# Four states of 32 channels on the partitions in a selective scan, with dense weights streamed

## The chip, the cores and the metric

The kernel runs on one core of one Trainium2 chip. The core has five engines, each with its own in-order queue: TensorE (PE), VectorE (DVE), ScalarE (ACT), GpSimd (POOL) and SyncE (SP), which here issues every DMA. A wait at the head of a queue holds everything behind it. The metric is device time in microseconds (us) of one execution. All data are float32.

## The reference

Eight images of 256 channels and 32x32 pixels (N = 1024 positions) go through four residual layers, each behind a group norm `_gn` (32 groups). Layer 0 is attention with 8 heads of 64; layers 1 and 2 are 3x3 convolutions 256 to 256; layer 3 is the long one. Cut to what matters:

```python
x = x + _L0_conv_ref(_gn(x), w_qkv, w_out, b_out)   # attention, q and k of unit length
x = x + _L1_conv_ref(_gn(x), scale, sign_w, bias)   # 3x3 conv
x = x + _L2_conv_ref(_gn(x), kernel, bias)          # 3x3 conv
x = x + _L3_conv_ref(_gn(x), ...)
# inside layer 3, xs = _gn(x) as positions x channels
xn = layernorm(xs)                  # over the 256 channels of a position
xc = four branches of 64 channels of xn
def mamba(xs):                      # one branch: 64 in, 128 inner channels, 16 states
    u, z = split(xs @ inw.T)
    u = silu(causal_conv4(u))
    xdbc = u @ xpw.T                # 4 columns for dt, 16 for B, 16 for C
    dt = softplus(xdbc[..., :4] @ dtw.T + dtb)
    # for every inner channel d and state s, along the 1024 positions:
    #   h[d,s] = exp(dt[d] * A[d,s]) * h[d,s] + dt[d] * u[d] * B[s]
    #   y[d]   = sum over s of h[d,s] * C[s]
    y = selective_scan(u, dt, B, C, -exp(alog), D)   # y + u * D
    return (y * silu(z)) @ outw.T
xm = mamba(xc) + skip * xc
# gate from two small convs and a sigmoid; depthwise and pointwise convs (r, then x2);
# attention with 8 heads of 32 over x2; a 512-to-256 projection, layernorm, gelu;
# normalisation, depthwise 3x3, layernorm, projection
```

The scan is the part that the change rewrites: 4 branches x 128 channels x 16 states, each a recurrence over 1024 positions, for 8 images.

## The kernel before

**Tiling.** Channels lie on the 128 partitions, positions along the free dimension. All weights are loaded once and stay in SBUF (`weight`, L72). Work tiles of 128x1156 come from one pool of 20 buffers (`work`, L46). In PSUM [...] two `big` tiles and one `acc` tile take two banks each, two `mm` tiles one bank each. The framework places semaphores itself; an instruction waits for the data it reads, and for the readers of the buffer that it takes over.

**Order.** A Python loop over the images (L938) emits `layer0` to `layer3` for one after another, with the next image's `x` loaded early (L942). Dense products go by halves of 512 positions: `project` (L248) and `conv3x3` (L523 on) fill one `mm` tile per half and output block, and evacuate it. `layer_norm` (L177) takes the mean with a matmul by a constant matrix, subtracts, squares on ACT, sums the squares over channels with 16 matmuls whose stationary operand has 8 columns (L196), then Sqrt on ACT and reciprocal on DVE, a matmul that broadcasts the result (L211), and two multiplications per half.

**The scan** is `mamba` (L562 on), once per branch. Its front: in-projection, causal conv on DVE (L588, L597), silu, projection to B, C and dt (L606), softplus (L622 to L629), du = dt*u (L631). B is stored to DRAM (L611). Then for each of the 16 states, with all 128 inner channels on the partitions and all 1024 positions in one tile:

1. `hs` is loaded with one row of B, broadcast to 128 partitions (L638, SP);
2. ACT computes `da` = exp(dt*A) (L641);
3. TensorE broadcasts the state's row of C into a `big` tile, by a matmul with one column of the weights repeated 128 times (L646);
4. GpSimd multiplies `hs` by du (L653);
5. DVE runs the recurrence in `hs` (L662) and multiplies it by C from PSUM (L663);
6. TensorE adds the result into `acc` by a matmul with the identity (L665).

`spread(s + 1)`, steps 1 to 4 of the next state, is emitted ahead of the scan of state s. At the end come y + u*D (L672), the gate (L676, L677), the output matmul (L680) and the skip (L683). A branch's front isn't emitted before the branch ahead of it has ended.

Of the kernel before, what the change touches and what calls it, by code (L numbers as in the profile page):

```python
# [26 lines left out]

@with_exitstack
def preact_stack(ctx: ExitStack, tc: tile.TileContext, I, out, cols):

# [5 lines left out]
    wp = ctx.enter_context(tc.tile_pool(name="wp", bufs=1))  # L36
    xp = ctx.enter_context(tc.tile_pool(name="xp", bufs=2))
    vp = ctx.enter_context(tc.tile_pool(name="vp", bufs=1))
    tp = ctx.enter_context(tc.tile_pool(name="tp", bufs=20))
    sp = ctx.enter_context(tc.tile_pool(name="sp", bufs=2))  # L40
    ps_big = ctx.enter_context(tc.tile_pool(name="ps_big", bufs=2, space=PSUM))
    ps_acc = ctx.enter_context(tc.tile_pool(name="ps_acc", bufs=1, space=PSUM))
    ps_mm = ctx.enter_context(tc.tile_pool(name="ps_mm", bufs=2, space=PSUM))
    dp = ctx.enter_context(tc.tile_pool(name="dp", bufs=2, space=DRAM))

    def work(name):  # L46
        return tp.tile([P, TW], F32, tag="t", name=name)

    def mm_tile():
        return ps_mm.tile([P, HALF], F32, tag="mm", name="mm")  # L50
# [4 lines left out]
    def acc_tile():  # L55
        return ps_acc.tile([P, N], F32, tag="acc", name="acc")

    def load_x(b):
        xt = xp.tile([P, 2, N], F32, tag="x", name="xt")
        nc.sync.dma_start(out=xt, in_=x_in[b].rearrange("(t p) n -> p t n", p=P))  # L60
        return xt


    x_next = load_x(0)
# [7 lines left out]
    def weight(name, parts=P):  # L72
        src = I[name]
        k = src.shape[0] // parts
        t = wp.tile([parts, k] + list(src.shape[1:]), F32, name="w_" + name)
        for i in range(k):
            nc.sync.dma_start(out=t[:, i], in_=src[i * parts : (i + 1) * parts])
        return t

    wqkv = weight("wqkv")  # L80
    wout = weight("wout")
    wc1 = weight("wc1")
    wc2 = weight("wc2")
    minw = weight("minw")
    mxpw = weight("mxpw")
    moutw = weight("moutw")
    mdtw = wp.tile([36, NB, P], F32, name="mdtw")
    nc.sync.dma_start(out=mdtw[32:36], in_=I["mdtw"])
    rpw = weight("rpw")
    fpw = weight("fpw")  # L90
    ainw = weight("ainw")
    aout = weight("aout")
    fcw = weight("fcw")
    projw = weight("projw")
# [6 lines left out]
    make_identity(nc, ident)  # L101

# [16 lines left out]
    var_w = wp.tile([P, NKT, NKT], F32, name="var_w")  # L119
    nc.gpsimd.memset(var_w, 0.0)  # L120
    for i in range(NKT):
        nc.gpsimd.memset(var_w[:, i, i : i + 1], 1.0 / C)
# [8 lines left out]
    a_neg = wp.tile([P, NB * DS], F32, name="a_neg")  # L131
    nc.scalar.activation(a_neg, vec[:, cols["alog"] : cols["alog"] + NB * DS], AF.Exp)
    nc.vector.tensor_scalar_mul(a_neg, a_neg, -1.0)

    def rsqrt_of(t, eps):

        nc.vector.tensor_scalar_add(t, t, eps)
        nc.scalar.activation(t, t, AF.Sqrt)
        nc.vector.reciprocal(t, t)
# [11 lines left out]
    def group_norm(xt, dsts, view=lambda a: a):  # L151
        mv = channel_stats([xt[:, t] for t in range(2)])
        pg = mm_tile()
# [3 lines left out]
        g = sp.tile([P, 2, 2], F32, tag="g", name="g")  # L157
# [4 lines left out]
        pd = mm_tile()  # L162
        nc.tensor.matmul(pd[:, 0:2], gmat, d, start=True, stop=True)
        rs = sp.tile([P, 2], F32, tag="rs", name="rs")
        nc.vector.tensor_add(rs, g[:, :, 1], pd[:, 0:2])
        rsqrt_of(rs, 1e-5)
# [10 lines left out]
    def layer_norm(srcs, dsts, finish):  # L177

        sq = []
        for t in range(2):  # L180
            sq.append(work("ln_sq"))
        for h in range(2):
            pm = mm_tile()
            for t in range(2):
                nc.tensor.matmul(
                    pm, mean_w, srcs[t][:, HALVES[h]], start=t == 0, stop=t == 1
                )
            for t in range(2):
                nc.vector.tensor_sub(dsts[t][:, HALVES[h]], srcs[t][:, HALVES[h]], pm)
                nc.scalar.activation(  # L190
                    sq[t][:, HALVES[h]], dsts[t][:, HALVES[h]], AF.Square
                )
        pv = mm_tile()
        for i in range(NKT):
            for t in range(2):
                nc.tensor.matmul(  # L196
                    pv[0:NKT, 0:P],
                    var_w[:, i],
                    sq[t][:, i * P : (i + 1) * P],
                    start=i == 0 and t == 0,  # L200
                    stop=i == NKT - 1 and t == 1,
                )
        rs = sp.tile([NKT, P], F32, tag="ln_rs", name="ln_rs")
        nc.vector.tensor_scalar_add(rs, pv[0:NKT, 0:P], 1e-5)
        nc.scalar.activation(rs, rs, AF.Sqrt)
        nc.vector.reciprocal(rs, rs)
        for h in range(2):
            pr = mm_tile()
            for i in range(4):
                blk = h * 4 + i  # L210
                nc.tensor.matmul(  # L211
                    pr[:, i * P : (i + 1) * P],
                    ident[0:NKT, blk : blk + 1].to_broadcast([NKT, P]),
                    rs,
                    start=True,
                    stop=True,
                )
            for t in range(2):
                part = dsts[t][:, HALVES[h]]
                nc.vector.tensor_mul(part, part, pr)  # L220
                finish(t, part)

# [25 lines left out]
    def project(w, srcs, evac):  # L248

        last = len(srcs) - 1  # L250
        for m in range(2):
            for h in range(2):
                ps = mm_tile()
                for k, src in enumerate(srcs):
                    nc.tensor.matmul(  # L255
                        ps,
                        w[:, k, m * P : (m + 1) * P],
                        src[:, HALVES[h]],
                        start=k == 0,
                        stop=k == last,  # L260
                    )
                evac(m, HALVES[h], ps)

    def attention_exact(heads):
# [25 lines left out]
        def transposes(u):  # L290
            ps = acc_tile()
# [8 lines left out]
        def values(u):  # L300
            head, qt = u["head"], u["qt"]
            if qt % 4 == 0:
                head["acc"] = mm_tile()
# [23 lines left out]
    def note(sums):  # L327
# [3 lines left out]
        nc.vector.tensor_reduce(chk[:, 0, at : at + 1], sums, axis=AX.X, op=ALU.min)  # L331
        nc.vector.tensor_reduce(chk[:, 1, at : at + 1], sums, axis=AX.X, op=ALU.max)

    def attention(pairs, add_up):
# [4 lines left out]

        def scores(u):  # L340
            pair, h, kt, n = u["pair"], u["h"], u["kt"], u["n"]
            s = acc_tile() if n % 3 == 2 else big_tile()
# [12 lines left out]
        def values(u):  # L355
            pair, h, kt = u["pair"], u["h"], u["kt"]
            if kt == 0:
                pair["acc"] = mm_tile()
# [20 lines left out]
            {"pair": pair, "h": h, "kt": kt} for pair in pairs for h in range(2) for kt in range(NKT)  # L379
        ]  # L380
        for n, u in enumerate(units):
            u["n"] = n
        for n in range(len(units) + 2):
            for stage, at in ((scores, n), (values, n - 2)):
                if 0 <= at < len(units):
                    stage(units[at])


    def layer0(xt, exact=False):
        xn = [work("xn0"), work("xn1")]  # L390
        group_norm(xt, [t[:, 0:N] for t in xn])

        v = vp.tile([P, NKT, 512], F32, tag="v", name="v")

        def values(kt):
            ps = mm_tile()
            for c in range(2):
                nc.tensor.matmul(
                    ps,
                    xn[c][:, kt * P : (kt + 1) * P],  # L400
                    wqkv[:, c, 1024:1536],
                    start=c == 0,
                    stop=c == 1,
                )
            nc.vector.tensor_copy(v[:, kt], ps)

        def rows_of(first, name):

            a = work(name)
            ss = sp.tile([P, 2], F32, tag="ss", name="ss", bufs=4)  # L410
            for h in range(2):
                ps = mm_tile()
                for c in range(2):
                    nc.tensor.matmul(  # L414
                        ps,
                        wqkv[:, c, first : first + P],
# [4 lines left out]
                nc.vector.tensor_copy(a[:, HALVES[h]], ps)  # L421
            sq = work("sq")
            nc.scalar.activation(
                sq[:, 0:N], a[:, 0:N], AF.Square, accum_out=ss[:, 0:1]
            )
            nc.scalar.activation(ss[:, 1:2], ss[:, 0:1], AF.Sqrt)
            nc.vector.tensor_scalar_max(ss[:, 1:2], ss[:, 1:2], 1e-12)
            nc.vector.reciprocal(ss[:, 1:2], ss[:, 1:2])
            return a[:, 0:N], ss[:, 1:2]

        qs, ks = [], []
        for t in range(4):
            q, rq = rows_of(t * P, "q")
            k, rk = rows_of(512 + t * P, "k")
            nc.vector.tensor_scalar(q, q, rq, 10.0, ALU.mult, ALU.mult)
            nc.vector.tensor_scalar_mul(k, k, rk)
            qs.append(q)
            ks.append(k)
            for kt in (2 * t, 2 * t + 1):
                values(kt)  # L440
# [3 lines left out]
        def heads():  # L444
            for t in range(4):
                o.append(work("o"))
                for e in range(2):
                    yield head(t, e)

        def head(t, e):  # L450
# [3 lines left out]
            def take(half, acc):  # L454
# [3 lines left out]
                "q": qs[t][rows],  # L458
# [606 lines left out]
```

## Time and profile before

| | us |
|---|---|
| median of 2 runs | 9570.62 (9567.94 to 9573.3) |
| profiled execution, its own time | 9565.23 |
| its span, first to last instruction | 9563.5 |
| one image to the next | 1195 |
| of that: layer 0, from its first statistics to the first conv | 211 |
| layers 1 and 2 (two convs) | 140 |
| norm and layer norm at the head of layer 3 | 16 |
| four branches of the scan | 531 |
| the rest of layer 3 | 299 |

The stages are those of image 1, cut at the first instruction of each, with some us of overlap at the seams; their sum is 1197. The largest groups outside the lines shown with the prediction:

| line, engine | what | instructions | busy us | mean ns |
|---|---|---|---|---|
| L665 PE | y += hs by the identity | 2048 records | 1211.6 | 726 |
| L360 PE | attention, values | 4096 records | 1098.0 | 617 |
| L646 PE | C broadcast | 2048 records | 1076.3 | 655 |
| L533 PE | 3x3 convs | 2304 records | 1033.5 | 612 |
| L641 ACT | exp(dt*A) | 512 | 563.7 | 1142 |
| L374 DVE | attention, sum of the exponentials | 384 | 470.5 | 1225 |

A float32 matmul leaves two records[...]. Busy time of PE overlaps with its weight loads (PEld), so the two aren't added. In a line of the profile, `hs<-a,hs 128x1024` names output and inputs and the shape in partitions x elements; "idle before" is the time that the engine stood still just before it, with what ended it.

### The profile page before, as it was taken

The numbers are of one execution on the slowest core, as the hardware profiler recorded it, in microseconds if no ns is written. First come the engines' busy times: TensorE is split into PE (matmuls) and PEld (weight loads), VectorE is DVE, ScalarE is ACT, GpSimd is POOL, SyncE is SP. The second block draws the span as 40 slices with busy tenths as digits, with TensorE's granted clock in tenths as the row PEclk, the third lists the DMA queues.
The fourth block names the chain that finished last, engine by engine and source line by source line (L and its number), as shares of the span: only waits on it lengthen the run. The fifth ranks groups of instructions, "written<-read, shape, count | busy, mean of one in ns | idle before, by whom it ended". The sixth has DMA issues, their size and how long they took to land.

```text
span 9563.5 us, 51820 instructions
## 1 busy us (share of the span) xinstructions
PE 7354.8 (77%) x19650; PEld 2690.0 (28%) x19650; DVE 5074.7 (53%) x4146; ACT 2543.9 (27%) x2835; POOL 2190.2 (23%) x1021
## 2 busy tenths in 40 slices
PE   9767897678975789757897578976789757897577
PEld 2322233222332223322233222332223322233222
DVE  6466364663646636466364663646536465364653
ACT  3121331213312133121331213312133121331213
POOL 0253002530025300253002530025300252002520
PEclk9878998788987889878898788987889878898788
DMA  1111001110012100121001210012100121001210
GB/s 51 36 64 42 0 9 36 69 38 2 8 36 69 38 0 9 36 69 38 3 7 36 69 38 5 5 36 71 36 9 0 36 71 36 5 1 36 71 36 5
DMA packets 86139, 300.76 MB, mean 31 GB/s; under 512 B 9844, under 2 KB 12532, under 8 KB 85368
## 3 DMA queue, kind: packets, MB, share of 16 engines
q1 hardware_dynamic: 85880, 297.36, 9.1%
q8 instruction: 156, 2.56, 0.1%
q14 instruction: 103, 0.84, 0.0%
HBM read 286.83 MB, written 10.49 MB: 31 GB/s over the span
## 4 chain that ended last, share of the span: by engine, by line
PE 59%; DVE 23%; issue 9%; POOL 4%; ACT 4%; DMA 0%; DVEq 0%; POOLq 0%; ACTq 0%
PE mm L533 11%; PE mm L360 10%; DVE hs L662 10%; PE big L344 7%; PE acc L665 5%; PE mm L255 4%; PE big L646 4%; PE acc L344 4%; PE mm L414 3%; DVE hs L663 2%; POOL hs L653 2%; DVE u L597 1%; DVE dw L920 1%; PE mm L606 1%; PE mm L716 1%
## 5 line engine op out<-in xcount | busy, mean ns | idle before, releaser
L665 PE MATMUL acc<-hs,ident 128*128 128x512 f32 x2048 | 1211.6, 726 | 1257.2 <-DVE hs L663 1256.9
L653 POOL TENSOR_TENSOR hs<-a,hs 128x1024 f32<-128x1024 f32 x512 | 1887.5, 3715 | 250.5 <-DMA hs<-b_rows 230.2
L662 DVE TENSOR_TENSOR_SCAN hs<-da,hs 128x1024 f32<-128x1024 f32 x512 | 1826.0, 3598 | 219.6 <-POOL hs L653 204.4
L360 PE MATMUL mm<-p,v 128*64 128x512 f32 x4096 | 1098.0, 617 | 0.0
L646 PE MATMUL big<-u,w_mxpw 128*128 128x512 f32 x2048 | 1076.3, 655 | 0.0
L533 PE MATMUL mm<-im,w_wc 128*128 128x512 f32 x2304 | 1033.5, 612 | 29.2 <-DVE im L168 25.6
L641 ACT ACTIVATE da<-dt,a_neg 128x1024 f32<-128x1024 f32 x512 | 563.7, 1142 | 1648.0 <-DVE hs L662 1460.9
L352 ACT ACTIVATE p<-big 128x1024 f32<-128x1024 f32 x688 | 702.4, 1023 | 1014.4 <-PE big L344 1013.4
L665 PEld LDWEIGHTS acc<-hs,ident 128*128 128x128 f32 x2048 | 437.2, 224 | 1894.3 <-DVE hs L663 1447.0
L663 DVE TENSOR_TENSOR hs<-hs,big 128x1024 f32<-128x1024 f32 x512 | 616.8, 1207 | 422.6 <-PE big L646 415.5
L344 PE MATMUL big<-q,k 32*128 32x512 f32 (+1 forms) x2752 | 772.1, 639 | 0.0
L646 PEld LDWEIGHTS big<-u,w_mxpw 128*128 128x128 f32 x2048 | 455.3, 224 | 650.8 <-issue 650.8
L533 PEld LDWEIGHTS mm<-im,w_wc 128*128 128x128 f32 x2304 | 450.4, 196 | 600.4 <-issue 600.4
L762 DVE COPY o<-mm 32x512 f32<-32x512 f32 x128 | 87.6, 684 | 879.6 <-PE mm L360 838.1
L696 POOL MEMSET v<- 128x2048 f32 x8 | 14.4, 1804 | 2195.1 <-PE mm L360 2195.1
L374 DVE TENSOR_TENSOR p<-p 128x1024 f32<-128x1024 f32 x384 | 470.5, 1225 | 42.1 <-ACT p L352 3.0
L628 POOL TENSOR_TENSOR dt<-dt,e 128x1024 f32<-128x1024 f32 x32 | 74.8, 2338 | 1566.5 <-ACT dt L627 1566.5
L360 PEld LDWEIGHTS mm<-p,v 128*64 128x64 f32 x4096 | 205.4, 135 | 770.0 <-issue 655.5
L352 ACT ACTIVATE p<-acc 128x1024 f32<-128x1024 f32 x336 | 344.0, 1024 | 288.5 <-PE acc L344 287.1
L344 PE MATMUL acc<-q,k 64*128 64x512 f32 (+1 forms) x1344 | 377.5, 638 | 0.0
L514 POOL MEMSET dwim<- 128x34 f32 x16 | 2.0, 127 | 1579.2 <-ACT p L352 1557.2
L344 PEld LDWEIGHTS big<-q,k 32*128 32x128 f32 (+1 forms) x2752 | 208.1, 184 | 552.0 <-issue 519.5
(198 smaller groups left out, 6359.7 us busy)
## 6 DMA issues: line engine op xcount, KB each, us to landing
hs<-b_rows SPq DMA_DIRECT2D x512, 512.0 KB, 4.2
xt<-in_x SPq DMA_DIRECT2D x8, 1024.0 KB, 4.8
out<-xt SPq DMA_DIRECT2D x32, 256.0 KB, 2.0
w_wc<-in_wc SPq DMA_DIRECT2D x4, 1152.0 KB, 12.2
b_rows<-low SPq DMA_DIRECT2D x32, 64.0 KB, 1.9
w_wqkv<-in_wqkv SPq DMA_DIRECT2D x2, 768.0 KB, 7.0
w_ainw<-in_ainw SPq DMA_DIRECT2D x2, 384.0 KB, 4.5
w_wout<-in_wout SPq DMA_DIRECT2D x4, 128.0 KB, 7.3
```

Of the source, the lines that this page charges most:

```text
L255: nc.tensor.matmul(ps, w[:, k, m * P : (m + 1) * P], src[:, HALVES[h]], start=k == 0, stop=k == last,)
L344: nc.tensor.matmul(s[:, HALVES[e]], pair["k"][e][:, kt * P : (kt + 1) * P], pair["q"][e][:, HALVES[h]], start=True, stop=True,)
L352: nc.scalar.activation(p, s, AF.Exp)
L360: nc.tensor.matmul(pair["acc"][e * 64 : e * 64 + 64], pair["v"][e](kt), u["p"][:, HALVES[e]], start=kt == 0, stop=kt == NKT - 1,)
L374: nc.vector.tensor_add(pair["sum"], pair["sum"], u["p"])
L533: nc.tensor.matmul(image(ps), w[:, c, 3 * dy + dx, m * P : (m + 1) * P], im[c][:, 16 * h + dy : 16 * h + dy + 16, dx : dx + 32], start=n == 0,
L641: nc.scalar.activation(da[:, 0:N], dd, AF.Exp, scale=a_neg[:, i * DS + s : i * DS + s + 1])
L646: nc.tensor.matmul(c_all[:, HALVES[h]], mxpw[:, 0, i, at : at + 1].to_broadcast([P, P]), u[:, HALVES[h]], start=True, stop=True,)
L653: nc.gpsimd.tensor_mul(hs[:, 0:N], du[:, 0:N], hs[:, 0:N])
L662: nc.vector.tensor_tensor_scan(hh, da[:, 0:N], hh, 0.0, ALU.mult, ALU.add)
L663: nc.vector.tensor_mul(hh, hh, c_all)
L665: nc.tensor.matmul(y_acc[:, HALVES[h]], ident, hs[:, HALVES[h]], start=s == 0, stop=s == DS - 1,)
```

## The change

It does these things at once:

- **Scan.** A tile now holds 4 states x 32 channels on its 128 partitions and 512 positions. Per branch there are 2 halves h x 4 quarters of the states q x 4 groups of channels g. dt and du are stored to DRAM and read back four times each, once per state (`spread_channels`); B and C are stored too, and each row is broadcast to 32 partitions (`spread_states`). A column of `carry` takes the state from the first half to the second. `da` goes to PSUM. The product with C, which was DVE's, is GpSimd's now; the broadcast of C by TensorE is gone; the sum over four states is the matmul with `sel` (128x32).
- **Order.** `mamba` is split into generators: the next branch's front runs between the quarters of a branch's scans. The images follow one another as before (`drain`).
- **Weights.** Dense weights are no longer resident: `chunk` loads each block when it's used, into 8 buffers. The image is stored at the head of the scans and read back after them.
- **Buffers.** 13 work buffers (of 1026 elements) for the dense part and pools of their own for the scans (6, 20 of 128x512, 4). PSUM: two `big`, one `acc` of one bank, two `da`, one `y`. So attention has two score tiles for three and one accumulator for two.
- **Dense part.** Evacuations are 1024 wide; `layer_norm` takes the squares as stationary operand and sums them into columns; square roots with reciprocals become a power of -0.5 on GpSimd (`inverse_root`); silu and sigmoid are made of tanh. In layer 0, q and k of a pair of heads are projected eight steps ahead of their use, not all at first. The gate convs (L951) have one tile for both halves.

Lines of the changed kernel that the prediction names: branch front: L660 and L669 conv taps (DVE), L674 silu's product (DVE), L702 and L703 and L706 softplus (DVE), L704 Ln (ACT), L705 dt subtraction and L710 du (GpSimd). Scans: L754 exp (ACT), L758 and L765 the two products (GpSimd), L760 scan (DVE), L771 u*D + y (DVE). Branch back: L791 gate (DVE), L792 y*gate (GpSimd), L795 output matmul (PE), L799 skip (DVE). SP's stores: L708 dt, L712 du, L686 B and C.

The diff, cut to its core:

```diff
+    wsp = ctx.enter_context(tc.tile_pool(name="wsp", bufs=8))
-    tp = ctx.enter_context(tc.tile_pool(name="tp", bufs=20))
+    tp = ctx.enter_context(tc.tile_pool(name="tp", bufs=13))
...
+    mp = ctx.enter_context(tc.tile_pool(name="mp", bufs=6))
+    qp = ctx.enter_context(tc.tile_pool(name="qp", bufs=20))
+    ps_da = ctx.enter_context(tc.tile_pool(name="ps_da", bufs=2, space=PSUM))
+    ps_y = ctx.enter_context(tc.tile_pool(name="ps_y", bufs=1, space=PSUM))
...
+    def chunk(name, i):
+        src = I[name]
+        k, n = src.shape[2:]
+        t = wsp.tile([P, HALF], F32, tag="w", name="w")
+        t = t[:, 0 : k * n].rearrange("p (k n) -> p k n", n=n)
+        nc.sync.dma_start(out=t, in_=src[i])
+        return t
...
-    def rsqrt_of(t, eps):
-        nc.vector.tensor_scalar_add(t, t, eps)
-        nc.scalar.activation(t, t, AF.Sqrt)
-        nc.vector.reciprocal(t, t)
+    def inverse_root(t):
+        nc.gpsimd.tensor_tensor(t, t, minus_half[:, 0 : t.shape[1]], ALU.pow)
...
                 nc.tensor.matmul(
-                    pv[0:NKT, 0:P],
-                    var_w[:, i],
-                    sq[t][:, i * P : (i + 1) * P],
+                    pv[:, i : i + 1],
+                    sq[t][:, i * P : (i + 1) * P],
+                    mean_w[:, 0:1],
...
-            s = acc_tile() if n % 3 == 2 else big_tile()
+            s = big_tile()
...
-                pair["acc"] = mm_tile()
+                pair["acc"] = acc_tile()
...
+    def branch_scans(i, br):
+        u = br["u"]
+        carry = sp.tile([P, 16], F32, tag="carry", name="carry")
+        def spread_channels(name, g, half):
+            t = quarter(name)
+            for s in range(4):
+                nc.sync.dma_start(
+                    out=t[s * 32 : s * 32 + 32],
+                    in_=br[name][g * 32 : g * 32 + 32, half],
+                )
+            return t
+        def spread_states(first, half):
+            t = quarter("bc")
+            for s in range(4):
+                nc.sync.dma_start(
+                    out=t[s * 32 : s * 32 + 32],
+                    in_=br["bc"][first + s : first + s + 1, half].to_broadcast(
+                        [32, HALF]
+                    ),
+                )
+            return t
+        for h, half in enumerate(HALVES):
+            y = ps_y.tile([P, HALF], F32, tag="y", name="y")
+            dts, dus = {}, {}
+            for q in range(4):
+                b, c = spread_states(4 * q, half), spread_states(DS + 4 * q, half)
+                for g in range(4):
+                    if q == 0:
+                        dts[g] = spread_channels("dt", g, half)
+                        dus[g] = spread_channels("du", g, half)
+                    at = i * 16 + q * 4 + g
+                    da = da_tile()
+                    nc.scalar.activation(
+                        da, dts[g], AF.Exp, scale=a_neg[:, at : at + 1]
+                    )
+                    hs = quarter("hs")
+                    nc.gpsimd.tensor_mul(hs, dus[g], b)
+                    keep = carry[:, q * 4 + g : q * 4 + g + 1]
+                    nc.vector.tensor_tensor_scan(
+                        hs, da, hs, 0.0 if h == 0 else keep, ALU.mult, ALU.add
+                    )
+                    if h == 0:
+                        nc.vector.tensor_copy(keep, hs[:, HALF - 1 : HALF])
+                    nc.gpsimd.tensor_mul(hs, hs, c)
+                    nc.tensor.matmul(
+                        y[g * 32 : g * 32 + 32], sel, hs, start=q == 0, stop=q == 3
+                    )
+                if q < 3:
+                    yield
+            nc.vector.scalar_tensor_tensor(
+                u[:, half], u[:, half], half_d[:, i : i + 1], y, ALU.mult, ALU.add
+            )
+            yield
...
+    def scan_layers(img):
...
+        for _ in branch_front(0, xn, br):
+            yield
+        for i in range(NB):
+            nxt = {}
+            front = branch_front(i + 1, xn, nxt) if i + 1 < NB else iter(())
+            for _ in branch_scans(i, br):
+                next(front, None)
+                yield
+            for _ in front:
+                pass
+            branch_back(i, xn, br)
+            yield
+            br = nxt
...
     for b in range(batch):
...
+        img = {}
+        drain(front_layers(image_of(b), img), scan_layers(img), back_layers(img, out[b]))
```

## The prediction

> **What bounds the kernel now.** The page first: the profiled execution took 9565.23 us (span 9563.5), 0.06% under the median 9570.62, so sums are made against it.
>
> ```profile
> PE 7354.8 (77%) x19650; PEld 2690.0 (28%) x19650; DVE 5074.7 (53%) x4146; ACT 2543.9 (27%) x2835; POOL 2190.2 (23%) x1021
> PE 59%; DVE 23%; issue 9%; POOL 4%; ACT 4%; DMA 0%; DVEq 0%; POOLq 0%; ACTq 0%
> ```
>
> The chain is mostly TensorE, then the scans (L662). One image repeats every 1195 us, so I cut image 1 by the first instructions of its stages and asked for busy times there:
>
> ```profile
> 1196.00:1407.00 211.00, 201.64 (x690) 62.02 (x688) 146.10 (x162) 83.70 (x100) 2.33 (x9) 0.99 0.03 10
> 1563.00:2094.00 531.00, 331.75 (x592) 127.76 (x592) 350.28 (x177) 125.02 (x125) 263.48 (x85) 0.77 0.19 64
> 2094.00:2393.00 299.00, 246.99 (x833) 83.60 (x833) 118.83 (x137) 101.90 (x118) 0.81 (x10) 0.89 0.01 2
> ```
>
> Columns: stretch, length, busy time of PE, weight loads, DVE, ACT, POOL, each with its count, then clock, DMA share, GB/s. The dense stretches are PE's. The scan stretch, 531 us of 1195, is nobody's alone. By line, in that stretch:
>
> ```profile
> L653 POOL TENSOR_TENSOR hs<-a,hs x64: 2335/4327/4398, 1594.0 to 2051.7; 128x1024 f32<-128x1024 f32 x64
> L662 DVE TENSOR_TENSOR_SCAN hs<-da,hs x64: 2258/3289/4424, 1596.4 to 2057.3; 128x1024 f32<-128x1024 f32 x64
> L663 DVE TENSOR_TENSOR hs<-hs,big x64: 1186/1220/1224, 1600.9 to 2083.5; 128x1024 f32<-128x1024 f32 x64
> ```
>
> Min/median/max ns: product and scan, both reading two SBUF tensors, nearly double when they meet; L663, which reads PSUM, never does. So about 4.4 us per state, then TensorE's 3.43 us per state when it catches up, and some 40 us of front and back per branch: 133 us a branch.
>
> [...] the trace, by the 2338 ns of L677 for 1024 columns and the 1264 of L549 for 512, has (2338-1264)/512 = 2.1 ns. [...] the 64 KB store b_rows<-low lands in 1.9 us.
>
> **The change, part by part.** The changed kernel's instruction lists show no image overlapping another; only the next branch's front is woven into a branch's scans.
>
> Outside fences, L660 to L799 from here on are lines of the changed kernel, listed with the change, but for the old L662, L663 and L677.
>
> *Products and scans.* Per branch 32 groups of 128x512 (two halves of time, four quarters of the states, four groups of channels), each with two products (L758, L765) and a scan (L760). What one product costs[...]:
>
> ```profile
> L549 POOL TENSOR_TENSOR xt<-xt,y x32: 1259/1264/1272, 236.5 to 8634.8; 128x512 f32<-128x512 f32 x32
> ```
>
> The scan: [...] 1186 - (2258-1186) = 0.11 us is fixed, and 512 columns take (2.26-0.11)/2+0.11 = 1.2 us; its da now lies in PSUM, so it stays off the lock. ACT's exp (0.6 us, as its other 128x512 rows) and the scan run beside GpSimd, which gets 64 x 1.26 = 80.6 us per branch against 16 x 2.34 = 37: the new bound. Gone are TensorE's 32 broadcasts of C and DVE's 16 L663 per branch; TensorE keeps 32 matmuls with sel, beside the products. GpSimd's list has, in the first quarter of each half, product, product of the same group, in turn: the second waits for the scan between. A group there costs 1.26+1.2+1.26+0.13 = 3.85, four 15.4. In the other quarters four and four follow one another: 8 x 1.26 = 10.1. A half is 15.4+30.3 = 45.7, a branch 91.4.
>
> *The woven front* (three of four branches). DVE's conv taps L660 (0.81, one source) and three L669, and L674 (1.28 each, two SBUF inputs), lock GpSimd out: 5.9 us. They stand in DVE's queue ahead of the second quarter's scans, for which GpSimd waits: 7 in all. At the half's end DVE's queue has L771 (u*D+y; it waits for y, so for the half's last product and its matmuls, 1.6) ahead of softplus's L702 and L703, which Ln waits for; and GpSimd's queue has the dt subtraction L705 and the du product L710 ahead of the second half's products. So 1.6+0.75+0.69+1.23+1.06, L705 2.34, DVE's L706 1.23, L710 2.35, and 0.9 for nine hand-overs of 0.1: 12.2 us. dt's store stands in SP's list among the next half's loads and waits for L706, du's for L710: groups 3 and 4 are loaded behind them, 16 x 0.32 and 2 us to land = 7.2 after L710, while the first two groups last 7.7: hidden.
>
> *The change of branch* (three times): y 1.6, L771 0.75, two gates L791 1.5, GpSimd's product L792 2.4, ahead of the next branch's first in its queue; then the first scan stands behind both L799, which wait for the output matmuls L795. After an idle stretch these are slow, as before:
>
> ```profile
> 2090.77 3.67 PE L680 MATMUL mm<-u,w_moutw 128*64 128x512 f32 x4 [3.86 <-POOL r L233]
> ```
>
> so 3.5+0.9, scan and second product 2.5, in sum 13.2; that group's 3.85 is counted above, which leaves 9.4.
>
> *Start and end.* Before, 31 us from the in-projection to the first product; dt and du now go through DRAM (1.9 to store, four loads and 2 us back) and one more L674: 38. End: y, L771, L792, matmuls, L799: 10. Slots: ten front matmul tiles per branch take turns with da in two PSUM banks: not shown before, 0 to 3 us each branch; I take 1.3.
>
> Sum: 38 + 4x91.4 + 3x(7+12.2) + 3x9.4 + 10 + 5 = 505 against 531: **-26 us** per image.
>
> *Operands.* SP issues 131 DMAs per branch (128 of 64 KB, three stores).
>
> ```profile
> L638 SPq DMA_DIRECT2D hs<-b_rows x64: 319/320/692, 1579.7 to 2047.8; - x64
> DMA to landing us min/median/max: 3.4/3.9/8.3
> ```
>
> At 0.32 us to issue, 42 us of the branch's 121: covered by the products. Bytes are the same as before.
>
> *LayerNorm's variance* (three per image). The squares become the stationary operand: 16 full weight loads instead of 16 of 8 columns.
>
> ```profile
> 1546.02 0.36 PE L154 MATMUL mm<-mv,gmat 128*128 128x4 f32 x2 [1.91 <-DVE mv L148]
> 1547.11 0.56 PE L163 MATMUL mm<-d,gmat 128*128 128x2 f32 x2 [0.74 <-DVE d L161]
> 2374.92 0.39 PE L196 MATMUL mm<-ln_sq,var_w 128*8 128x128 f32 x2 [0.64 <-ACT ln_sq L190]
> ```
>
> Warm 0.36, cold 0.56: 16 take some 7 us against 3.9; the broadcast 3.6 against 1.0 before its first use; whole-width steps lose the overlap of halves, 3 us. Two whole-width at +8.5, one by halves at +4: +21. All on the path: nothing else runs there.
>
> *Rest of the dense part.* Full-width evacuations at each stage's end (1.28 for 0.75, L549's add 2.34 for 1.26, two bn_stats): +5. Attention: the first q/k pair's copy, square and scale are no longer behind other matmuls, +5; 13 buffers for 20, 0 to 6, taken 3; one accumulator for two, so that the second attention's first value matmul waits for four copies (2.9 us in the trace, half covered by two score tiles): 8 x 1. Gates: six of twelve L951 run early, -5. Weights streamed: eight chunks ahead of matmuls of 5.2 us per chunk against 3 to 5 us to land: nothing, as long as SP isn't held up. Power on GpSimd for Sqrt and reciprocal: not in the trace; between a memset's 0.13 us and a full product's 1.26, against 0.65 replaced, nine times on the path: -5 to +5, taken 0. Sum with 1 for odds: **+38**.
>
> Net +12 per image, x8 = 96: 9565+96 = 9661, median 5 more: **9670**.
>
> **Rivals.** *A, slower: operands bound the products.* Each load waits for the eighth before it. If the longest landing seen, 8.3 us, becomes the rule, 8.3/8 = 1.04 us per DMA: 131 take 136 us per branch. It decides above 121/131 = 0.92. Stage: 38+4x136+10 = 592, so 8x(61+38) = +790: 10,360. For: loads gather at each half's start, SP's list mixes them with stores that wait for DVE and GpSimd. Against: a median of 3.9 gives 0.49.
>
> *B, faster: GpSimd's dispatch overlaps.* Of 1.26 us only 1.07 grows with size; back to back, 64 x 0.19 = 12 us less per branch, and DVE's locks fall into waits: -70 per image, LayerNorm half as dear -10: 8x(12-80) = -544: 9030. For: memsets start 0.03 us apart though each lasts 0.10. Against: product and scan alternate, so dispatch is exposed in a quarter of the groups.
>
> *C: it doesn't do what it says*, the lock remaining with da in PSUM: scan and product then exclude each other again, up to 32 x 1.2 = 38 us per branch, 1220 in all: 10,890. L663's steady 1.19 to 1.22 speaks against it.
>
> **Numbers.** Forecast 53%: its own range, stage 485 to 530 and dense +25 to +50, is 9,400 to 9,960, mostly within 2% (0.33), sometimes slower (0.17) or faster (0.03). A 26%, B 17%, C 4%. So faster 0.20, same 0.33, slower 0.47; 2% is about what runs of this kernel tell from no change. The range, 9,030 to 10,450, takes in half of B and most of A and leaves out the rest and C, about 0.2.
>
> **What would show it.** Scan stage near 505 us, GpSimd the busiest engine there; the second product waiting for DVE's scan in the first quarters only; GpSimd's waits of some 6 us before the dt subtraction and 4 before L792; products at 1.26, scans at 1.2 us. A shows as GpSimd waiting for DMA. I'm wrong if products last over 1.5 us, the dense stretches grow by over 60 us, or an image overlaps the next.

## The result and the profile after

The changed kernel takes 9636.42 us (median of 2 runs, 9634.88 to 9637.95) against 9570.62: ratio 1.0072, interval 1.0047 to 1.0096, so 0.7% slower. The profiled execution took 9637.95 (span 9636.1), 72.7 more than that of before. First the page: busy times by engine, and the chain by engine.

```profile
PE 6672.0 (69%) x17602; PEld 2099.6 (22%) x17602; DVE 4004.4 (42%) x4259; ACT 2523.5 (26%) x3097; POOL 3014.4 (31%) x2661
PE 32%; POOL 12%; DVE 10%; issue 7%; SPq 4%; ACT 3%; DMA 2%; POOLq 0%; DVEq 0%; ACTq 0%
```

TensorE and DVE have 680 and 1070 us less to do, GpSimd 820 more, and the time is nearly the same: a sum of work says nothing here, only the stages do. The chain's shares sum to 70% only, because it could be followed back no further than 2,872 us. Of what it covers, TensorE has 46% (59 before) and GpSimd 17% (4 before). Busy times by stage for image 1, with cuts that both kernels have (first matmul of the q, k and v projections, of the convs, of the first layer norm, of the first branch; the last output matmul; the next image), the changed kernel first:

```profile
1218.15:1430.05 211.90, 197.81 (x677) 59.78 (x676) 135.81 (x123) 85.47 (x105) 6.84 (x10) 0.98 0.05 15
1430.05:1573.94 143.89, 130.56 (x297) 57.57 (x297) 12.87 (x27) 2.41 (x2) 7.49 (x21) 0.94 0.14 40
1573.94:1590.89 16.95, 14.84 (x56) 10.89 (x56) 4.69 (x8) 3.32 (x6) 1.64 (x1) 0.60 0.31 122
1590.89:2093.73 502.84, 235.54 (x345) 36.37 (x344) 228.83 (x256) 131.51 (x179) 354.66 (x275) 0.62 0.29 76
2093.73:2419.97 326.24, 254.82 (x829) 97.58 (x830) 117.90 (x118) 92.76 (x96) 5.97 (x27) 0.85 0.03 9
```

The same cuts in the kernel before:

```profile
1203.60:1408.27 204.67, 196.96 (x677) 59.85 (x677) 143.23 (x155) 83.57 (x99) 2.33 (x9) 0.99 0.02 6
1408.27:1549.40 141.13, 130.86 (x296) 57.67 (x296) 14.31 (x33) 3.51 (x6) 5.85 (x21) 0.95 0.00 0
1549.40:1563.19 13.79, 11.32 (x56) 6.71 (x56) 6.05 (x10) 3.63 (x7) 0.00 (x0) 0.87 0.00 0
1563.19:2090.77 527.58, 328.52 (x589) 127.02 (x589) 349.34 (x176) 124.83 (x124) 263.33 (x83) 0.78 0.19 64
2090.77:2396.92 306.15, 251.22 (x841) 84.93 (x841) 122.08 (x147) 102.11 (x119) 0.96 (x15) 0.89 0.01 4
```

The second figure of a row is its length. Layer 0 is 7.2 us longer, the convs 2.8, the first layer norm 3.2, the scans **24.7 shorter**, the back 20.1 longer: +8.5 per image, 68 in eight. In the scans GpSimd is now the busiest engine, 355 of 503 us. The scans by line (min/median/max ns), with both forms of the scan, since in the second half it starts from `carry`:

```profile
L758 POOL TENSOR_TENSOR hs<-du,bc x128: 1252/1263/2252, 1627.0 to 2079.1; 128x512 f32<-128x512 f32 x128
L760 DVE TENSOR_TENSOR_SCAN hs<-da,hs x64: 1192/1223/1226, 1628.3 to 2035.1; 128x512 f32<-128x512 f32 x64
L760 DVE TENSOR_TENSOR_SCAN hs<-da,carry,hs x64: 1276/1283/1284, 1695.8 to 2080.4; 128x512 f32<-128x512 f32 x64
```

The second product, L765, is like the first: 1257/1264/2299. Compare the spread of before, 2258 to 4424 for the scan: with da in PSUM a scan keeps its 1.22 us, or 1.28 from `carry`, whatever GpSimd does. Twelve of the 256 products take 2.2 to 2.3 us, four per woven front: those that met the next branch's conv and silu on DVE.

### The profile page after: what moved, and what is told of

The parts are those of the page before. It is cut to its first block, busy times and chain, and to the rows that moved or that the text cites. A ratio compares the mean times of both kernels' runs of the same rounds, so it can differ in the third digit from the quotient of the medians.

```text
span 9636.1 us, 56994 instructions
## 1 busy us (share of the span) xinstructions
PE 6672.0 (69%) x17602; PEld 2099.6 (22%) x17602; DVE 4004.4 (42%) x4259; ACT 2523.5 (26%) x3097; POOL 3014.4 (31%) x2661
## 3 DMA queue, kind: packets, MB, share of 16 engines
q1 hardware_dynamic: 273496, 416.10, 15.3%
## 4 chain that ended last, share of the span: by engine, by line
PE 32%; POOL 12%; DVE 10%; issue 7%; SPq 4%; ACT 3%; DMA 2%; POOLq 0%; DVEq 0%; ACTq 0%
POOL hs L758 7%; PE acc L420 7%; PE big L602 7%; PE big L404 6%; SPq L726 4%; POOL hs L765 3%; PE big L305 3%; DMA bc<-bc 2%; DVE hs L760 1%; PE y L766 1%; DVE dw L1070 1%; PE big L867 1%; PE acc L242 1%; PE big L484 1%; PE da L695 1%
## 5 line engine op out<-in xcount | busy, mean ns | idle before, releaser
L766 PE MATMUL y<-hs,sel 128*32 128x512 f32 x2048 | 1342.2, 963 | 1616.0 <-POOL hs L765 1614.9
L765 POOL TENSOR_TENSOR hs<-hs,bc 128x512 f32<-128x512 f32 x1024 | 1319.1, 1311 | 591.7 <-DVE carry L764 403.1
L412 ACT ACTIVATE p<-big 128x1024 f32<-128x1024 f32 x1024 | 1046.9, 1023 | 1385.8 <-PE big L404 1340.9
L758 POOL TENSOR_TENSOR hs<-du,bc 128x512 f32<-128x512 f32 x1024 | 1316.2, 1309 | 67.1 <-DMA du<-du_m 34.5
L754 ACT ACTIVATE da<-dt,a_neg 128x512 f32<-128x512 f32 x1024 | 705.3, 691 | 1906.3 <-DVE hs L760 1242.8
L420 PE MATMUL acc<-p,v 128*64 128x512 f32 x4096 | 1102.7, 625 | 65.3 <-ACT rs L919 65.3
L602 PE MATMUL big<-im,w 128*128 128x512 f32 x2304 | 1029.2, 610 | 31.0 <-issue 31.0
L760 DVE TENSOR_TENSOR_SCAN hs<-da,carry,hs 128x512 f32<-128x512 f32 x512 | 638.8, 1283 | 746.6 <-POOL hs L758 686.6
L760 DVE TENSOR_TENSOR_SCAN hs<-da,hs 128x512 f32<-128x512 f32 x512 | 614.8, 1216 | 634.2 <-POOL hs L758 605.6
L404 PE MATMUL big<-q,k 64*128 64x512 f32 x2048 | 589.9, 657 | 62.6 <-DVE k L495 37.7
L404 PE MATMUL big<-qk,qk 32*128 32x512 f32 x2048 | 562.1, 635 | 2.6 <-DVE qk L875 2.6
```

The costliest lines, as they stand in the source:

```text
L404: nc.tensor.matmul(s[:, HALVES[e]], pair["k"][e][:, kt * P : (kt + 1) * P], pair["q"][e][:, HALVES[h]], start=True, stop=True,)
L412: nc.scalar.activation(p, s, AF.Exp)
L420: nc.tensor.matmul(pair["acc"][e * 64 : e * 64 + 64], pair["v"][e](kt), u["p"][:, HALVES[e]], start=kt == 0, stop=kt == NKT - 1,)
L602: nc.tensor.matmul(image(ps[:, HALVES[h]]), w[:, dx], im[c][:, 16 * h + dy : 16 * h + dy + 16, dx : dx + 32], start=n == 0, stop=n == 17,)
L754: nc.scalar.activation(da, dts[g], AF.Exp, scale=a_neg[:, at : at + 1])
L758: nc.gpsimd.tensor_mul(hs, dus[g], b)
```

## Experiments

All are edits of the changed kernel, and "against 9,636" means that kernel's time. Its own ratio to the kernel before has an interval of 0.25% to each side, so differences under some 30 us aren't read as such.

**The lock.** `da_sbuf`:

```diff
-                    da = da_tile()
+                    da = half_work("da")
```

> The changed kernel with one edit: the scan's da lies in an SBUF tile instead of PSUM. Theory[...]: a scan with two SBUF inputs and a GpSimd product exclude each other for their whole length, so in the second to fourth quarters each of the 12 groups of a half pays the scan, 1.22 us, on top of two products; 12 x 1.22 = 14.6 us per half, 117 per image, 8 images: 9636 + 940 = about 10,575, with scans or products that last up to twice 1.22 us. Rival (the place of da doesn't matter, GpSimd is simply slow): 9,640, products and scans unchanged.

10,244 us, ratio 1.0701 (1.0684 to 1.0719): +608. The lock, by which a scan of two SBUF tiles and a GpSimd product that meet both take longer, is there, at two thirds of the size. Its scans, and GpSimd's work in a last quarter:

```profile
L760 DVE TENSOR_TENSOR_SCAN hs<-da,hs x64: 1212/2217/2269, 1711.7 to 2175.9; 128x512 f32<-128x512 f32 x64
...
1960.40 6.77 POOL L758 TENSOR_TENSOR hs<-du,bc 128x512 f32<-128x512 f32 x4
1967.14 6.75 POOL L765 TENSOR_TENSOR hs<-hs,bc 128x512 f32<-128x512 f32 x4
```

In the whole run the 256 scans of first quarters, where product and scan alternate, keep their time; the other 768 all take longer, 736 of them over 2 us. Eight products take 13.5 us in a last quarter instead of 9.8. That is 3.7 per quarter where four full exclusions, 4.9, were expected: each scan costs GpSimd some 0.9 us and not 1.22, so the exclusion isn't quite for the whole length, as was expected. What makes the two exclude each other no run shows.

**Who does the second product.** `c_dve`:

```diff
-                    nc.gpsimd.tensor_mul(hs, hs, c)
+                    nc.vector.tensor_mul(hs, hs, c)
```

> The changed kernel with one edit: the second product, by C, is done by DVE instead of GpSimd. Theory (GpSimd's two products per group bound the scans): DVE then carries scan 1.22 and product 0.69 (as its other 128x512 product of two SBUF tiles) and in half of the groups the carry copy 0.15, some 2.1 us per group with hand-overs, GpSimd one product of 1.22 and the time it is locked out; 32 x 2.1 = 67 us per branch against 90.8 measured, so 32 branches x -24 = -760: about 8,880. Rival (every DVE product has to wait for a whole GpSimd product, so scan, product and product follow one another): 3.1 us per group, 100 per branch, +300: about 9,930.

9,171 us, ratio 0.9579 (0.9563 to 0.9595): -465, faster than both kernels. So GpSimd's products bounded the scans. 300 us of the expected gain are missing. DVE is now the busiest engine of the scans, 322 of 444 us in image 1, with GpSimd at 206. Waits in that kernel's scans (us in total, times, longest) show where some of it went:

```profile
DVE hs L760 <- POOL hs L758: 48.0, 16, 10.2
POOL hs L758 <- DMA du<-du_m: 41.0, 15, 5.9
```

Per image GpSimd waits 41 us for du, against 1.6 before this edit, and DVE 48 us for GpSimd's products. The steady part did better than expected: when the products have run ahead, four scans and four products take DVE 4.8 + 2.5 us, 1.8 per group.

**What then is late.** `c_dve_stores`, on top of `c_dve`:

```diff
-        nc.sync.dma_start(out=br["dt"], in_=dd)
+        nc.gpsimd.dma_start(out=br["dt"], in_=dd)
...
-        nc.sync.dma_start(out=br["du"], in_=aa)
+        nc.gpsimd.dma_start(out=br["du"], in_=aa)
```

> The second product on DVE, and in addition the stores of dt and du issued from GpSimd's queue instead of SP's. Theory (with faster groups the loads of the second half's operands are no longer covered: in the run with the product on DVE, GpSimd waits 10.7 us per branch for du at the start of a second half, behind the two stores in SP's queue, which wait for DVE and GpSimd): 10.7 us less for three branches per image, less some 2 us for issuing on GpSimd, 8 images: -200, about 8,970 against 9,171. Rival (the loads wait for their landing or for free buffers, not for the stores): 9,171.

9,085 us, ratio 0.9491 (0.9475 to 0.9507): -87 against `c_dve`, less than half of what was expected. Its waits:

```profile
DVE hs L760 <- POOL hs L758: 31.5, 8, 11.8
POOL hs L758 <- DMA du<-du_m: 21.0, 7, 6.3
POOL hs L758 <- PE y L766: 41.7, 12, 6.7
```

The stores were half of the wait for du. On GpSimd the 20 us came again elsewhere: ten as waits for rows of B and C (16.5 against 6.7), next in SP's queue, and twelve as waits for a buffer that y's matmuls still read (41.7 against 29.9). A wait of GpSimd costs time here only where DVE waits for it in turn. DVE's wait for the products fell by 16.5 us, and the image by 11 (87/8).

**The half boundary.** `early` takes away the pause after the in-projection in the front, so that all its later steps come a quarter of the states earlier:

```diff
             nc.scalar.copy(raw[:, 3 + h * HALF : 3 + (h + 1) * HALF], ps)
-        yield
```

> The changed kernel with one edit: the next branch's front has no pause between in-projection and conv, so that all its later steps come a quarter earlier, and Ln for softplus runs during the last quarter's scans instead of after u*D + y. Theory (GpSimd stands 6 us before the dt subtraction only because the softplus stands behind y): this wait goes, at some cost for a DVE operation on two SBUF tiles of 1.23 us that now locks GpSimd among products: -5 us, three branches, 8 images: -120, about 9,515. Rival (the wait only moves, to the du product, which waits for DVE's maximum behind u*D + y, or to the exponentials behind two table loads): 9,600 to 9,640.

9,665 us, ratio 1.0094 (1.0077 to 1.0111): no gain, and by the intervals no clear loss. That lies outside both expectations, nearer to the rival. GpSimd in the changed kernel, from the start of the last two quarters before a boundary:

```profile
1662.40 4.93 POOL L758 TENSOR_TENSOR hs<-du,bc 128x512 f32<-128x512 f32 x4
...
1688.51 2.34 POOL L705 TENSOR_TENSOR dt<-dt,e 128x1024 f32<-128x1024 f32 x1 [6.16 <-ACT dt L704]
1692.18 2.34 POOL L710 TENSOR_TENSOR a<-dt,u 128x1024 f32<-128x1024 f32 x1 [1.34 <-DVE dt L706]
```

and in `early`:

```profile
1666.87 4.94 POOL L758 TENSOR_TENSOR hs<-du,bc 128x512 f32<-128x512 f32 x4
...
1690.60 2.34 POOL L705 TENSOR_TENSOR dt<-dt,e 128x1024 f32<-128x1024 f32 x1
1694.60 2.34 POOL L710 TENSOR_TENSOR a<-dt,u 128x1024 f32<-128x1024 f32 x1 [1.67 <-DVE dt L706]
1698.86 1.26 POOL L758 TENSOR_TENSOR hs<-du,bc 128x512 f32<-128x512 f32 x1 [1.92 <-DMA du<-du_m]
```

The bracket is the idle time before an instruction and who ended it. The 6.16 us are gone, as the theory said. But the last two quarters take 23.7 us instead of 20.0, and 1.9 us of waiting for du's load are new. The rival's own reason, the du product L710, hardly shows: it waits 1.67 us instead of 1.34. In the scans of an image DVE waits 23.5 us for da, against 1.0 in the changed kernel: the front's matmuls and da take turns in two PSUM banks, and the earlier front probably meets more scans there. From the first branch's in-projection to L792 of the last one, both kernels need 500 us in image 1.

**One accumulator.** `acc2`:

```diff
-                pair["acc"] = acc_tile()
+                pair["acc"] = da_tile()
```

> The changed kernel with one edit: the attention's accumulator comes from the pair of PSUM tiles that hold da in the scans, so that there are two in turn. Theory (one accumulator stalls the values' matmuls): TensorE's seven waits for the copies, 8.1 us per image in the profile, go: 8 x -8 = -65, about 9,570. Rival (ScalarE, with exponentials and copies, sets the pace, and the stall is where its lag shows): within 15 us of 9,636.

9,575 us, ratio 1.0005 (0.9996 to 1.0014): -62. The changed kernel's waits of TensorE have this line, and in `acc2` it is gone:

```profile
PE acc L420 <- ACT rs L919: 8.1, 7, 1.2
```

**Layer norm, by form and by width.** `ln_var` puts the old form of the variance back, `ln_half` the old width of the last two layer norms (with tiles of the da pool for `big` ones):

```diff
-                    pv[:, i : i + 1],
-                    sq[t][:, i * P : (i + 1) * P],
-                    mean_w[:, 0:1],
-                    start=t == 0,
-                    stop=t == 1,
+                    pv[0:NKT, 0:P],
+                    var_w[:, i],
+                    sq[t][:, i * P : (i + 1) * P],
+                    start=i == 0 and t == 0,
+                    stop=i == NKT - 1 and t == 1,
...
-        inverse_root(r)
+        nc.scalar.activation(r, r, AF.Sqrt)
+        nc.vector.reciprocal(r, r)
...
-                    r[:, i : i + 1].to_broadcast([P, P]),
-                    ident,
+                    ident[0:NKT, i : i + 1].to_broadcast([NKT, P]),
+                    r,
```

> The changed kernel with the layer norms' variance in its old form: weights of 8 columns as stationary operand, the squares moving, square root on ScalarE and reciprocal on DVE, broadcast from 8 partitions. Theory (full weight loads of the squares, the wide broadcast and the power of 8 columns are what makes a layer norm dearer): per layer norm 5.2 to 6.6 us of matmuls become 3.9, a broadcast of 3.8 becomes 2.1, the power's 1.9 becomes 1.6: -4.5, three per image, 8 images: -105, about 9,530. Rival (the width of the steps is the cause, this form costs nothing): 9,636.

```diff
-    WHOLE = ((slice(0, N), big_tile),)
+    WHOLE = tuple((h, da_tile) for h in HALVES)
```

> The changed kernel with one edit: the last two layer norms of an image go by halves, as its first does, instead of at full width. Theory (at full width subtraction, square, product and affine no longer overlap across halves): 3 to 5 us for each of the two, 8 images: -50 to -80, about 9,570. Rival (only the form of the variance matters): 9,636.

`ln_var` 9,617 us, ratio 1.0044 (1.0027 to 1.0060): -19, within the uncertainty of zero. It changes matmul, root and broadcast together, so only their sum is tested. Its last layer norm, up to the projection, takes 27.5 us in some images and 23.3 in others. `ln_half` 9,518 us, ratio 0.9944 (0.9926 to 0.9963): -118. So the width counts and the form, as a whole, hardly. An image's last layer norm at full width, in the changed kernel:

```profile
2386.79 5.96 PE L229 MATMUL big<-dw,mean_w 128*128 128x512 f32 x8 [28.39 <-DVE dw L1070]
...
2396.35 6.56 PE L242 MATMUL acc<-mean_w,ln_sq 128*128 128x1 f32 x30 [0.61 <-ACT ln_sq L238]
...
2411.30 8.83 PE L305 MATMUL big<-dw,w 128*128 128x512 f32 x16 [2.54 <-ACT dw L274]
```

by halves, in `ln_half`:

```profile
2362.77 5.80 PE L229 MATMUL da<-dw,mean_w 128*128 128x512 f32 x8 [27.19 <-DVE dw L1070]
...
2368.41 3.92 PE L242 MATMUL acc<-mean_w,ln_sq 128*128 128x1 f32 x32
...
2378.08 7.13 PE L305 MATMUL big<-dw,w 128*128 128x512 f32 x16 [0.18 <-ACT dw L274]
```

From the first mean matmul to the projection 24.5 us against 15.3. The 32 records with full weight loads last 3.9 us by halves, as the old form did before; at full width they take 7.1 us, and the old form at full width takes 6.7 (`ln_var`). The clock granted to TensorE differs there. The same stretches, with length, PE's busy time, granted clock, DMA share and GB/s, first at full width:

```profile
2395.10:2402.95 7.85, 7.15 (x32) 0.50 0.00 0
```

and by halves:

```profile
2368.41:2372.33 3.92, 3.82 (x33) 1.00 0.00 0
```

During the mean matmuls just ahead the clock is about 0.6 in both (0.61 at full width). What differs after them is that TensorE stands still for 2.4 and 0.6 us at full width and not at all by halves. So in these traces gaps of that size between short bursts go with half the clock, 0.50 against 1.00; that they cause it no run shows.

**The power on GpSimd.** `no_pow`:

```diff
-        nc.gpsimd.tensor_tensor(t, t, minus_half[:, 0 : t.shape[1]], ALU.pow)
+        nc.scalar.activation(t, t, AF.Sqrt)
+        nc.vector.reciprocal(t, t)
```

> The changed kernel with one edit: each power of -0.5 on GpSimd is a square root on ScalarE and a reciprocal on DVE again. Theory (the exchange costs nothing on balance): the powers of 8 columns, 1.64 us, lose some 1 us three times per image, those of 1 or 2 columns 0.2 us some six times, and table loads of 1.28 us come back, two or three of them on the path: within 40 us of 9,636. Rival (the power is dear, and the layer norms' growth is its doing): 9,560 or less.

9,732 us, ratio 1.0162 (1.0145 to 1.0179): +96, outside both expectations. Groups of ScalarE's table loads in one image of this kernel (count, busy us, mean ns, idle time before):

```profile
L175 ACT ACT_TABLE_LOAD x9 | 11.5, 1283 | 0.2
L412 ACT ACT_TABLE_LOAD x7 | 9.0, 1283 | 0.1
```

TensorE's largest wait in its layer 0 (us in total, times, longest), which the changed kernel doesn't have:

```profile
PE big L404 <- ACT p L412: 8.3, 3, 2.8
```

The changed kernel has one load at L412 and none for roots. Layer 0 takes 224.6 us instead of 211.9, the rest of the image 2 us less. There, q and k are normalised between the exponentials of the attention, so that a root after exponentials is preceded by a table load, and the next exponential by another. A load takes 1283 ns, and ScalarE stands still for only 0.2 us in all before the nine at L175 and 0.1 before the seven at L412. Layer 0 has 14 loads instead of one and is 12.7 us longer, 1.0 for each added load; 8.3 of it are the wait above.

**Streamed weights.** `chunks2`:

```diff
-    wsp = ctx.enter_context(tc.tile_pool(name="wsp", bufs=8))
+    wsp = ctx.enter_context(tc.tile_pool(name="wsp", bufs=2))
```

> The changed kernel with 2 weight buffers instead of 8. Theory (streamed weights cost nothing because a chunk of 192 KB lands in 2.3 us while the matmuls of one chunk last 5.2): even one chunk ahead suffices, within 60 us of 9,636. Rival (it is the lead of eight chunks that hides them): some 50 chunks per image, each exposed for 2 us, +800: 10,400.

9,669 us, ratio 1.0103 (1.0086 to 1.0120): +33, near the limit of what these runs tell. One chunk ahead nearly suffices. With eight buffers the list of TensorE's waits has none for a weight chunk; with two, its matmuls wait 0.7 us per image for one and its weight loads 2.5.

**Together, and woven.** `best_seq` is `c_dve`, `acc2` and `ln_half` in one.

> Three edits together in the changed kernel, images in sequence: second product on DVE, two accumulators for the attention, the last two layer norms by halves. Theory (they lie in different stages and so add up): -465, -62 and -118 from 9,636: 8,990. Rival (they share slack: a shorter stage meets a colder TensorE or waits for loads): 9,050 or more.

8,981 us, ratio 0.9385 (0.9370 to 0.9401): the three add up to within 10 us.

`woven` changes the order of the images alone, cut to its core:

```diff
-    for b in range(batch):
-        img = {}
-        drain(front_layers(image_of(b), img), scan_layers(img), back_layers(img, out[b]))
+    def weave(scan, dense, steps=44, load=620.0):
+        done = 0.0
+        for n, _ in enumerate(scan):
+            while done < load * (n + 1) / steps:
+                cost = next(dense, None)
...
+                done += cost
...
+    for b in range(batch):
...
+            beside.append(back_layers(imgs[b - 1], out[b - 1]))
...
+            beside.append(front_layers(image_of(b + 1), imgs[b + 1]))
+        weave(scan_layers(imgs[b]), chain(*beside))
```

> The changed kernel with another order: while image b is in its scans, the back of image b-1 and the front of image b+1 are emitted between the scans' steps; nothing else is changed. Theory (with the scans on GpSimd and TensorE at 3 per cent work there, the dense part can run beside them): per image TensorE's some 750 us become the bound, with collisions on DVE[...] 800 to 950, plus the first front and the last back, 700: 7,000 to 7,800. Rival (queues in order tie the two together and DVE's dense work locks GpSimd out): 9,300 or more.

7,455 us, ratio 0.7787 (0.7764 to 0.7810). `woven_c` adds the edit of `c_dve`.

> The woven order (back of image b-1 and front of image b+1 between the scans of image b) with the second product on DVE. Theory (woven, TensorE is the bound at 83 per cent, and GpSimd's products matter only where scans lag): GpSimd's load falls by 1,400 us in all, DVE's rises by 700; between -250 and 0 from 7,455: 7,200 to 7,455. Rival (DVE, which then carries the dense part and both scan steps, becomes the bound and its two-input products lock GpSimd out): 7,500 to 7,900.

7,329 us, ratio 0.7658 (0.7643 to 0.7673), the fastest here, 23% under the kernel before. Busy time by engine over its span:

```profile
PE 6112.6 (83%) x17602; PEld 2025.1 (28%) x17602; DVE 4754.1 (65%) x5283; ACT 2472.8 (34%) x3097; POOL 1891.2 (26%) x1637
```

TensorE is by far the busiest again, and has 48% of the chain; DVE has 25%. The edit on the second product is worth 126 us here and 465 in sequence: what shortens the scans counts less once they lie beside other work.

## Why the prediction was right

Forecast 9,670, measured 9,636: two terms that nearly cancel, and both came near. Some of that nearness is luck, since errors in single steps cancel too: start and halves came out below the forecast, front, change of branch and end above it. By steps, in us, measured in image 1 (a half is one of the last branch, where no front is woven in, its first without the late first scan):

| step | forecast | measured |
|---|---|---|
| scan stage against before | -26 | -24.7 |
| start | 38 | 36.1 |
| a half | 45.7 | 45.4 and 45.5 |
| woven front, three times | 7 | 10 |
| half boundary, three times | 12.2 | 12.1, 11.8, 11.8 |
| change of branch, three times | 9.4 | 9.6, 10.3, 10.0 |
| end, to the last L799 | 10 | 12.9 |
| front's turns with da in PSUM | 5 | inside the woven front |
| whole stage, to the last L799 | 505 | 507 |
| dense part | +38 | +33.2 |
| three layer norms | +21 | 3.2 + 9.7 + 10.0 |
| one accumulator | +8 | 7.7 (62/8, `acc2`) |
| weights streamed | 0 | no wait; two buffers 33/8 = 4 (`chunks2`) |

**Scan stage.** The mechanism was right: GpSimd's products set the pace, and the waits stand where they were put. A product lasts 1.26 us and comes every 1.22, so 0.04 of the 0.19 that rival B would hide are hidden. The scan's fixed 0.11 us, from which the forecast has its 1.2 us, was the author's estimate; by 2258 ns for 1024 columns (the least in the kernel before) and 1223 for 512 it is 0.19. A group of the first quarter takes 4.0 us in the first half (the carry copy, 0.15, was left out) and 3.9 in the second, 3.85 in the forecast. The front was mis-sized: a half with it takes 55.4 us against 45.4. DVE in the changed kernel at the end of a first quarter, and GpSimd's product behind it:

```profile
1646.39 0.81 DVE L660 TENSOR_SCALAR u<-u_raw,vec 128x1024 f32<-128x1024 f32 x1 [4.89 <-ACT u_raw L656]
1647.12 0.15 DVE L764 COPY carry<-hs 128x1 f32<-128x1 f32 x1
1647.35 2.30 POOL L765 TENSOR_TENSOR hs<-hs,bc 128x512 f32<-128x512 f32 x1 [7.11 <-DVE carry L764]
```

The first tap waits for ScalarE's copy of the in-projection; the carry copy is queued behind the tap, and the product, which overwrites what the carry copy reads, behind that. This wait is 5.6 us over the usual 1.5. Ahead of it two in-projections of 2.07 us and two copies of 0.58 follow one another (the second in-projection waits for the first copy), in tiles of the da pool. As far as the trace tells, it is a matter of the turns in PSUM, which the forecast put at 1.3 us per branch. The lock, put at 5.9, adds 4: four products of 2.2 to 2.3 us instead of 1.26, which meet L669 and L674. That L660, 0.8 of the 5.9, locks too is not shown: it meets no product in the whole run. The wait at the half boundary is where the prediction put it, 6.16 us before L705; taking it away brought nothing (`early`).

**Dense part.** The sum was near and one of its reasons wrong. The layer norms' +21 was put mainly on full weight loads of the squares on a TensorE partly at a lower clock (granted 0.84 in the matmuls that the prediction calls warm, 0.50 in the cold ones), 7 us against 3.9, and the wide broadcast, with 3 us for the lost overlap of halves. The 7 us came, but not because of the loads: without them it is 6.7 at full width (`ln_var`), with them 3.9 by halves (`ln_half`). At full width TensorE idles, for 2.4 and 0.6 us, and then runs at half the clock, 0.50; by halves the last two layer norms are 6.8 and 9.2 us shorter. "Power on GpSimd 0" holds outside layer 0 (2 us less without it); in layer 0 the power saves the table loads of the interleaved projection of q and k, 12.7 us, which the sum never set against the interleaving's cost. No run undoes the interleaving itself. The first q/k pair's +5 is in layer 0's +7.2 (TensorE waits 4.7 us for k). The rest of that, and the convs' 2.8, no run takes apart. Not foreseen: the next image's statistics and group norm now run beside the last layer norm, which saves 4.8 us from the last projection's first matmul to the next image's. In this small way an image does overlap the next, one of the prediction's own signs of being wrong.

**Rivals.** A: the operand loads land in 2.0 to 2.1 us, not 8.3, and GpSimd waits 8.5 us per image for DMA in the scans. SP needs 0.42 us and not 0.32 to issue one, 55 us of a branch's 126, still covered. Its premise holds: of the 380 DMAs of the kernel before that the trace lets one test, none is issued before the eighth ahead of it has landed, though 13 are before the seventh has. A wasn't absurd: with the second product on DVE, the loads at a half's start are at once what GpSimd waits for. C: the scans' 1.22 us rule it out, and `da_sbuf` shows what it would have cost, 608 us and not the 1220 of the forecast, since the first quarters' scans meet no product and each of the others costs 0.9 us and not 1.2.

## What to carry over

Before operations are moved to another engine, sum its work per group and not only what the old engine is rid of: here 32 products of 1.22 us, 39 us per branch, came on top of the 32 that GpSimd had already, to relieve a DVE whose scans the operand in PSUM had freed of the lock (median 1.22 us, against 2.22 in `da_sbuf`). Price a step by the stage around it: here 32 records of matmuls behind idle stretches took 7.1 us instead of 3.9, and roots between exponentials 12.7 us in layer 0, more by their place than by their size. And engines freed in one stage bring little until other work is put there: the order of the images was worth 2,180 us, the best edit inside a stage 465.

## What the runs showed of the hardware

- GpSimd's power takes 0.54 us for 1 column of 128 partitions, 0.70 for 2 and 1.64 for 8: about 0.16 per column, far more than a product's 0.0021.
- The same 32 records of 128x1 matmuls take 3.9 us, at a granted clock of 1.00, on a TensorE that is busy for 5.6 us before them without a gap, and 7.1 us, at 0.50, with idle stretches of 2.4 and 0.6 us ahead.
- A DVE product of two SBUF tiles among GpSimd's products keeps its 0.69 us in three of four cases (up to 1.80 at worst in `c_dve`), and its mean is 0.87; the mean of GpSimd's products rises from 1.31 to 1.42 (0.88 and 1.44 in `woven_c`). Both take longer beside each other.
- Issuing a 512 KB store takes 0.60 us of GpSimd's queue and 0.34 of SP's.
